# A graph attention layer on one core: q of the last node blocks made behind the first gathers, and a new order of the tail

## The chip, the cores and the metric

One core of a Trainium2 chip runs the whole kernel. The metric is the device time of one execution in microseconds (us). Engines are named as in the profile: PE is TensorE (matrix products and transposes), DVE is VectorE, ACT is ScalarE, POOL is GpSimd, SP is SyncE (it only issues DMAs here). The products are fp32; TensorE's granted clock is given as a share of full speed.

## What is computed

The reference, cut to what matters (12,500 nodes of 256 features, 8 heads of 32, 200,000 edges sorted by their destination `dst`):

```python
h = jnp.maximum(_layernorm(x, axis=-1), 0.0)
q = (h @ Wq + bq).reshape(n, HEADS, D)          # k and v alike
logits = einsum('ehd,ehd->eh', q[dst], k[src]) / sqrt(D)
seg_max = segment_max(logits, dst)
expv = exp(logits - seg_max[dst])
attn = expv / segment_sum(expv, dst)[dst]
agg = segment_sum(attn[:, :, None] * v[src], dst)
g = gelu(agg.reshape(n, HID) + (h @ Wskip + bskip))
y = h + g
out = x + layernorm(y) * gamma + beta
```

So every edge needs the k and v rows of its source, which lie anywhere, and the q row of its destination, which comes in order.

## The kernel before, in words

**Projection** (`project`, L157 to L280). The nodes make 98 blocks of 128, in groups of 1, 2, 4, then 5 for most of the way, and 4, 4, 2, 1 at the end. For each block: layer norm and relu give h; two transposes (L141) and ScalarE's copy to hT (L143); two products of 128x512 for k and v (L258) and their bias addition on VectorE (L261); two products of 128x256 for q (L264) and their bias addition (L268). q is kept as a rounded high part (L269, ScalarE) and the rest (L270, POOL). SP stores each group into three tables in DRAM: h_tab and kv_tab (L273), q_pc (L275). Between these steps VectorE makes a plan of the walk from `dst` (`make_plan`, its last operations L687 to L691).

**Walk over the edges** (`walk_streams`, L768 to L1507). The edges are cut into 8 streams, which advance side by side in NST = 66 steps; a step takes 3 tiles of 128 edges of each stream (the last step 2). Step c does this:

- `gather` (L1058): POOL issues one indirect DMA per stream and tile, 128 rows of kv_tab of 2 KB each: 24 in a step, 1576 in all. They go into tiles of two steps, `rows[c % 2]`; tiles are taken in an order of their own (`ORDER`, 1, 0, 2) when c % 4 is 2 or 3. The gathers of step c + 2 are issued during step c (`gather_next`) and are paced behind VectorE's operations.
- `windows` (L1044 to L1050): SP loads the q rows that the 8 streams can meet in this step from q_pc, at addresses read at run time, 8 loads. `prefetch` (L1030) and `penalties` (L1036) load the step's one-hot codes (et) and masks (pen).
- `hot_e` (L1075, L1077) makes 0/1 matrices of edges against window rows on TensorE and ScalarE, `spread` (L1098) multiplies them with the window, so that each edge has its q.
- On VectorE, `times` (L1107, in two halves) multiplies q by the gathered k, `total` (L1114) adds up over each head; `turn` (L1122, TensorE) turns the logits, `maxima` (L1133 to L1136) takes the segment maxima along the streams, `exponent` (L1140) is on ScalarE, `turn_back` (L1149) on TensorE. `weigh` (L1162 to L1169, VectorE) multiplies v by the weights: only then is a gathered tile free again.
- `hot_n` (L1086, L1088) and the sums (`add_up` and its parts, L1192 to L1216) add the weighted v per node on TensorE; they go to a table.

Pairs of node blocks whose edges are complete are finished meanwhile (`Pair`): `fetch` of sums, x and h; `turn` (L858, L861: h turned); `skip` (L874, L878: h times Wskip); `divide` (L850 to L867); `add` (L883); `gelu` (L887); `stats` (L890 to L896); `root` (L900); `factors` (L904, L905); `normal` (L910); `shifted` (L917, L920: the bias and x); `scale` (L924, L926); `store` by SP (L931) or `store_aside` by POOL (L938). Gelu and Sqrt need different tables of ScalarE; `table_of` (L1010) loads one.

**What sets the order.** In `walk_streams`, nearly every instruction goes through `keep`, which chains it behind the instruction kept before it on its engine. The order in the source is the order on each engine. Ahead of the loop over steps, the source issues the loads of et and pen for step 0, windows(0), the loads for step 1, the 24 gathers of step 0, windows(1), et of step 2, the 24 gathers of step 1, and then the work of step 0. The last two steps, a = 64 and b = 65, are written out after the loop (L1340 to L1496), with the pair blocks that remain: `older`, `before`, `pair` and `late` (class Pair), and four of class Last (`lasts`), which use free halves of gathered tiles as their room.

Of the kernel before, what the change touches and what calls it, by code (L numbers as in the profile page):

```python
# [71 lines left out]
def gnn_kernel(ctx: ExitStack, tc: tile.TileContext, x, src, dst, Wq, bq, Wk, bk, Wv, bv,  # L72
# [83 lines left out]

    def project():  # L157
# [8 lines left out]
        sizes = [1] * NBLK  # L166
        if NBLK >= 14:
            mid = NBLK - 14
            sizes = [1, 2, 4] + [5] * (mid // 5) + [mid % 5] * (mid % 5 > 0) + [4, 2, 1]
        with tc.tile_pool(name="proj_c", bufs=1) as cpool, \  # L170
# [16 lines left out]
            starts = [sum(sizes[:i]) for i in range(len(sizes))]  # L187
# [12 lines left out]
            qscale = 1.0 / math.sqrt(D)  # L200
# [33 lines left out]
            for g, (b0, n) in enumerate(zip(starts, sizes)):  # L234
# [18 lines left out]
                qp = pool.tile([P, 5, 2, HID], F32R, name="qp")[:, :n]  # L253
                for b in range(n):
# [6 lines left out]
                    nc.vector.tensor_tensor(kvo[:, b, :], ps_kv, b_kv, op=OP.add)  # L261
                    ps_q = psum.tile([P, HID], F32, name="ps_q", bufs=1)
# [9 lines left out]
                for tab, t in ((h_tab, h), (kv_tab, kvo)):  # L272
                    nc.sync.dma_start(tab[b0 * P:(b0 + n) * P, :]  # L273
                                      .rearrange("(p b) d -> p b d", p=P), t)
                nc.sync.dma_start(q_pc[b0 * P:(b0 + n) * P, :]  # L275
                                  .rearrange("(p b) d -> p (b d)", p=P),
                                  qp.rearrange("p b k d -> p (b k d)").bitcast(F32))
# [72 lines left out]
    with tc.If(fits > 0) as branch:  # L350
        table = dram.tile([S, NT, KV], F32, name="table")
        walk_streams(tc, N, HID, NST, KL, many, ident, idx, d0_row, slot_row, near, near_n, e_tab, pen_tab,
                     h_tab, kv_tab, q_pc, table, x, out, w_s, one_row, b_s3, b_o3, gam, eps)
    with branch.Else():
        gtab = dram.tile([NP + P, SUMS + HEADS], F32, name="gtab")
        q_tab = dram.tile([NP, HID], F32, name="q_tab")
        queries(q_tab)
# [65 lines left out]
def make_plan(tc, pool, ep, psum, src, dst, N, LEN, NST, SLACK, NT, dram, ident, flag, idx, d0_row,  # L423
# [9 lines left out]
    def behind(ins, share):  # L433

        tc.add_manual_dep(ins.ins, biased[len(biased) * share // 100].ins.name,
# [332 lines left out]
def walk_streams(tc, N, HID, NST, KL, many, ident, idx, d0_row, slot_row, near, near_n, e_tab, pen_tab, h_tab,  # L768
                 kv_tab, q_pc, table, x, out, w_s, one_row, b_s3, b_o3, gam, eps):
# [206 lines left out]
    with ExitStack() as es:  # L976
# [250 lines left out]
        prefetch(0)  # L1227
        penalties(0)
        windows(0)
        prefetch(1)  # L1230
        penalties(1)
        for c in range(2):
            for j in range(tiles_of(c)):
                gather(c, j)
            if c == 0:
                windows(1)
                prefetch(2)
# [132 lines left out]
        lasts = [last(rest[0], spare, 1, True), last(rest[1], kv[1], 0, False),  # L1370
# [37 lines left out]
        lasts[1].fetch_rows()  # L1408
        lasts[2].fetch_rows()
        for half in range(2):  # L1410
            times(b, 1, half)
        total(b, 1)
        pair.skip()
        turn(b, 1)
        weigh(a, 0)
        lasts[3].fetch_rows()
        late.turn()
        late.skip()
        weigh(a, 2)
        maxima(b)  # L1420
        add_up_products(a, 0, (0,))
        add_up_products(a, 1, (1, 0))
        exponent(b)
        before.stats()
        add_up(a, 0, (2,))
        add_up_products(a, 2, (1, 0))
        turn_back(b)
        add_up(a, 1, (2,))
        add_up(a, 2, (2,))
        carried(b)  # L1430
        for j in range(2):
            hot_n(b, j)
        lasts[0].turn()
        lasts[0].skip()
        weigh(b, 1)
        pair.divisors()
        pair.divide()
        pair.add()
        for i in range(3):
            add_up_products(b, i, (1,))  # L1440
        table_of(AF.Gelu)
        pair.gelu()
        weigh(b, 0)
        for i in range(3):
            add_up(b, i, (0,))
        for p in lasts:
            p.fetch_sums()
        late.divisors()
        late.divide()
        late.add()  # L1450
        late.gelu()
        pair.stats()
        lasts[1].turn()
        lasts[1].skip()
        late.stats()
        table_of(AF.Sqrt)
        ends = (before, pair, late)
# [4 lines left out]
        for p in ends:  # L1462
            p.normal()
        lasts[2].turn()
        lasts[2].skip()
        for i, p in enumerate(ends):
            p.shifted()
            p.scale()
            p.store_aside()
            if i == 0:  # L1470
                lasts[3].turn()
                lasts[3].skip()
# [379 lines left out]
```

## Time and profile before

| | us |
|---|---|
| runs shown | 2437.38, 2433.07, 2431.04 (median 2433.07) |
| profiled execution | 2429.78 |
| its span, first to last instruction | 2428.1 |
| TensorE, VectorE, ScalarE, POOL busy | 1697.2, 1996.9, 1061.4, 1664.4 |
| first gather starts, last gather starts | 338.75, 2334.74 |
| last gelu ends | 2402.36 |

The profile is that of one execution. It has a page of groups (engine, line, count, busy time, mean of one, and the idle time of the engine ahead of them with what ended it), slices of the span, and a chain of waits that is followed back from the last instruction. Timelines list start, length and instruction; "issue" is time in which an engine waited for nothing that the profile shows. x8 on a TensorE row counts records: an fp32 product has two. The row "POOLq" or "SPq" is the engine's sequencer, which issues DMAs.

### The profile page before, as it was taken

The numbers are of one execution on the slowest core, as the hardware profiler recorded it, in microseconds if no ns is written. First come the engines' busy times: TensorE is split into PE (matmuls) and PEld (weight loads), VectorE is DVE, ScalarE is ACT, GpSimd is POOL, SyncE is SP. The second block draws the span as 40 slices with busy tenths as digits, with TensorE's granted clock in tenths as the row PEclk, the third lists the DMA queues.
The fourth block names the chain that finished last, engine by engine and source line by source line (L and its number), as shares of the span: only waits on it lengthen the run. The fifth ranks groups of instructions, "written<-read, shape, count | busy, mean of one in ns | idle before, by whom it ended". The sixth has DMA issues, their size and how long they took to land.

```text
span 2428.1 us, 29469 instructions
## 1 busy us (share of the span) xinstructions
PE 1697.2 (70%) x7824; PEld 904.4 (37%) x7824; DVE 1996.9 (82%) x2461; ACT 1061.4 (44%) x2323; POOL 1664.4 (69%) x1751
## 2 busy tenths in 40 slices
PE   6999974555556766667667777676777677667685
PEld 3555532222233333333333333333333333334343
DVE  7579946777788888888988888888888888988873
ACT  4333322333334545545545545455454455455443
POOL 4433547777777777777777777777777777777730
PEclk9999975666667777766767767677677677776666
DMA  7776678888888888988888888888888889988961
GB/s 272 293 265 260 235 257 249 255 256 255 255 269 275 285 279 286 285 274 285 286 284 280 280 291 279 276 285 285 279 281 275 285 270 285 295 269 285 291 189 56
DMA packets 305551, 649.32 MB, mean 267 GB/s; under 512 B 52836, under 2 KB 191470, under 8 KB 300378
## 3 DMA queue, kind: packets, MB, share of 16 engines
q0 software_dynamic: 129056, 424.02, 55.7%
q1 hardware_dynamic: 175570, 222.67, 27.1%
q8 instruction: 64, 1.05, 0.2%
q14 instruction: 113, 0.93, 0.1%
q10 hardware_dynamic: 748, 0.66, 0.1%
HBM read 538.91 MB, written 108.23 MB: 267 GB/s over the span
## 4 chain that ended last, share of the span: by engine, by line
DMA 27%; PE 22%; DVE 18%; issue 12%; POOL 11%; ACT 7%; SPq 3%; DVEq 0%; another core or an unknown queue 0%; POOLq 0%; ACTq 0%
DMA kv<-kv_tab,idx 18%; POOL kv L1058 10%; PE ps_kv L258 5%; DVE kv L1107 4%; DVE vw L1162 4%; PE ps_a L878 4%; DVE L L1114 4%; PE ps_q L264 3%; DMA h<-h_tab 3%; PE ps_qe L1098 2%; DMA out_dram<-o 2%; PE ps_a L1192 1%; DMA sums<-table 1%; PE ps_hot L920 1%; SPq L845 1%
## 5 line engine op out<-in xcount | busy, mean ns | idle before, releaser
L1058 POOL DMA_INDIRECT kv<-kv_tab,idx x1576 | 1517.3, 963 | 482.6 <-issue 339.2
L1107 DVE TENSOR_TENSOR kv<-ps_qe,kv 128x1024 f32<-128x1024 f32 x394 | 470.7, 1219 | 213.8 <-DMA kv<-kv_tab,idx 140.3
L1114 DVE TENSOR_REDUCE L<-kv 128x64 f32<-128x2048 f32 x197 | 450.4, 2286 | 6.9 <-DVE kv L1107 0.2
L1162 DVE TENSOR_TENSOR vw<-ps_x,kv 128x2048 f32<-128x2048 f32 x197 | 449.4, 2281 | 3.6 <-PE ps_x L1149 2.7
L1098 PE MATMUL ps_qe<-qw,to_e 64*128 64x256 f32 (+1 forms) x1576 | 310.2, 392 | 108.9 <-DVE kv L1107 105.8
L1077 ACT ACTIVATE to_e<-ps_hot,ones 128x384 fp32r<-128x384 f32 x396 | 210.5, 573 | 316.3 <-PE ps_hot L1075 307.8
L1098 PEld LDWEIGHTS ps_qe<-qw,to_e 64*128 64x128 f32 (+1 forms) x1576 | 221.8, 246 | 274.4 <-DVE kv L1107 168.5
L1192 PE MATMUL ps_a<-vw,to_n 128*32 128x264 f32 (+1 forms) x2344 | 276.5, 504 | 0.0
L1122 PE MATMUL ps_x<-ident,L 128*64 128x128 f32 x197 | 72.7, 369 | 281.4 <-DVE vw L1169 210.7
L1206 ACT COPY sums_w<-ps_a 128x264 f32<-128x264 f32 x129 | 48.8, 379 | 482.1 <-PE ps_a L1192 426.7
L1075 PE MATMUL ps_hot<-et,near 48*128 48x384 bf16 x396 | 142.5, 420 | 126.8 <-ACT to_e L1077 122.3
L258 PE MATMUL ps_kv<-w_kv,hT 128*128 128x512 f32 x392 | 192.4, 612 | 16.0 <-ACT hT L143 15.0
L270 POOL TENSOR_TENSOR qp<-qp 128x256 fp32r<-128x256 f32 x98 | 96.3, 983 | 154.7 <-ACT qp L269 154.4
L878 PE MATMUL ps_a<-w_s,hT 128*128 128x256 f32 x352 | 164.6, 648 | 19.5 <-ACT hT L861 16.7
L1192 PEld LDWEIGHTS ps_a<-vw,to_n 128*32 128x32 f32 (+1 forms) x2344 | 99.6, 139 | 197.1 <-issue 161.4
L1122 PEld LDWEIGHTS ps_x<-ident,L 128*64 128x64 f32 x197 | 24.7, 126 | 374.6 <-DVE vw L1169 300.6
L1212 ACT COPY kv<-ps_a 1x264 f32<-1x264 f32 x388 | 143.0, 369 | 6.4
L1192 PE MATMUL ps_hot<-vw,to_n 128*64 128x264 f32 x808 | 139.4, 494 | 0.0
L878 PEld LDWEIGHTS ps_a<-w_s,hT 128*128 128x128 f32 x352 | 110.5, 329 | 65.7 <-ACT hT L861 41.8
L1010 ACT ACT_TABLE_LOAD x101 | 129.6, 1283 | 1.7
L1088 ACT ACTIVATE to_n<-ps_hot,ones 128x384 f32<-128x384 f32 x197 | 103.7, 578 | 53.4 <-PE ps_hot L1086 51.2
L264 PE MATMUL ps_q<-w_q,hT 128*128 128x256 f32 x392 | 103.1, 386 | 8.3 <-DVE qp L268 8.2
(288 smaller groups left out, 2111.8 us busy)
## 6 DMA issues: line engine op xcount, KB each, us to landing
qw<-q_pc SPq DMA_DIRECT2D x264, 128.0 KB
kv<-kv_tab,idx POOLq DMA_INDIRECT x1576
kv_tab<-kvo SPq DMA_DIRECT2D x16, 1280.0 KB
q_pc<-qp SPq DMA_DIRECT2D x16, 1280.0 KB
qw<-q_pc SPq DMA_DIRECT2D x264, 64.0 KB
table<-sums_w SPq DMA_DIRECT2D x260, 61.9 KB
pen<-pen_tab SPq DMA_DIRECT2D x66, 192.5 KB
sums<-table SPq DMA_DIRECT2D x90, 132.0 KB
```

Of the source, the lines that this page charges most:

```text
L258: ins = nc.tensor.matmul(ps_kv, hT[:, c, :], w_kv[:, c, :], start=c == 0, stop=c == KC - 1)
L264: ins = nc.tensor.matmul(ps_q, hT[:, c, :], w_q[:, c, :], start=c == 0, stop=c == KC - 1)
L878: self.keep(nc.tensor.matmul(self.ps[:, b, :], self.hT[:, b, c, :], w_s[:, c, :], start=False, stop=False, skip_group_check=True))
L1058: ins = keep(nc.gpsimd.indirect_dma_start(out=t[:, s, :], out_offset=None, in_=kv_tab[:, :], in_offset=bass.IndirectOffsetOnAxis(ap=idx[:, ...
L1075: keep(nc.tensor.matmul(ps[:, :CH], near[:, i * P:(i + 1) * P], step[c]["et"], start=True, stop=True))
L1077: keep(nc.scalar.activation(step[c]["to_e"][:, i, :], ps[:, :CH], AF.Relu, scale=-1.0, bias=ones))
L1098: keep(nc.tensor.matmul(ps[:, b, a, :], g["to_e"][at:at + w, i, j * P:(j + 1) * P], g["qw"][at:at + w, i, :], start=True, stop=True))
L1107: keep(nc.vector.tensor_tensor(k, g["qe", half].rearrange("p b a d -> p a b d"), k, op=OP.mult))
L1114: keep(nc.vector.tensor_reduce(g["L"][:, j, :].rearrange("p (s h) -> p s h", s=S), g["kv"][j][:, :, :HID].rearrange("p s (h d) -> p s h d" ...
L1162: keep(nc.vector.tensor_tensor(t[:, :, HEADS:].rearrange("p s (h d) -> p s h d", h=HEADS), wj[:, :, :, None].to_broadcast([P, S, HEADS, D] ...
L1192: keep(nc.tensor.matmul(ps[at:at + w, :], g["to_n"][:, j, i * P + at:i * P + at + w], g["vw"][j][:, s, :], start=j == turns(c)[0], stop=j ...
L1212: keep(nc.scalar.copy(step[c + 1]["kv"][0][0:1, s, HID - HEADS:], ps[at:at + 1, :]))
```

## The change

Two parts.

**A.** The products of q for the blocks from LATE on are taken out of `project`. A new function `late_queries` makes them inside `walk_streams`, after the 48 gathers of steps 0 and 1 have been issued: it loads Wq and bq again, and for each pair of blocks loads h from h_tab, turns it, multiplies, adds the bias, splits high part and rest, and stores both to q_pc. windows(0), windows(1) and prefetch(2) come after it; et and pen of steps 0 and 1 are loaded within it. It uses the room of the pairs (`sums`, `h`, `hT`, `x_f`, `o`) and the TensorE banks of `hot_e` and `spread`.

**B.** In the written-out tail, the weighings and sums of step a move ahead of the last products of step b; `pair.skip` and the turns and skips of `late` and `lasts` move behind the turned weights of b or behind b's sums; the pair `before` is finished earlier, with one more table load.

The diff, cut to its core (left out: the function's passing to the other branch of `tc.If`, the shifting of `sizes` and `starts`, and an index in the plan's order that stays the same):

```diff
+    LATE = next((b for b in starts if b >= NBLK - 24 and (NBLK - b) % 2 == 0), NBLK)
+    qscale = 1.0 / math.sqrt(D)
+    def late_queries(tile, transposed_ps, product_ps, keep, meanwhile=lambda: None):
+        w_q = tile("sums", KC * HID).rearrange("p (c n) -> p c n", c=KC)
+        b_q = tile("sums", HID)
+        keep(nc.sync.dma_start(w_q, Wq.rearrange("(c p) n -> p c n", p=P)))
+        keep(nc.sync.dma_start(b_q, bass.AP(tensor=bq.tensor, offset=bq.offset,
+                                            ap=[[0, P], [1, HID]])))
+        pairs = range(LATE, NBLK, 2)
+        def fetched(b0):
+            h = tile("h", 2 * HID).rearrange("p (b d) -> p b d", b=2)
+            keep(nc.sync.dma_start(h, h_tab[b0 * P:(b0 + 2) * P, :]
+                                   .rearrange("(p b) d -> p b d", p=P)))
+            return h
+        def transposes(h):
+            ps = transposed_ps()
+            for b in range(2):
+                for c in range(KC):
+                    keep(nc.tensor.transpose(ps[:, b, c, :], h[:, b, c * P:(c + 1) * P], ident))
+            return ps
+        ahead = [fetched(b0) for b0 in pairs[:2]]
+        meanwhile()
+        for t in (w_q, b_q):
+            keep(nc.vector.tensor_scalar(t, t, qscale, None, op0=OP.mult))
+        turned = [transposes(ahead.pop(0))] if ahead else []
+        for i, b0 in enumerate(pairs):
+            hT = tile("hT", 2 * KC * P).rearrange("p (b c d) -> p b c d", b=2, c=KC)
+            keep(nc.scalar.copy(hT, turned.pop()))
+            if i + 1 < len(pairs):
+                turned.append(transposes(ahead.pop(0)))
+            ps = product_ps()
+            for b in range(2):
+                for c in range(KC):
+                    keep(nc.tensor.matmul(ps[:, b, :], hT[:, b, c, :], w_q[:, c, :],
+                                          start=c == 0, stop=c == KC - 1))
+            hi = tile("x_f", 2 * HID).rearrange("p (b d) -> p b d", b=2)
+            lo = tile("o", 2 * HID).rearrange("p (b d) -> p b d", b=2)
+            keep(nc.vector.tensor_tensor(lo, ps, b_q[:, None, :].to_broadcast([P, 2, HID]),
+                                         op=OP.add))
+            keep(nc.scalar.copy(hi.bitcast(F32R), lo))
+            keep(nc.vector.tensor_tensor(lo.bitcast(F32R), lo, hi, op=OP.subtract))
+            if i + 2 < len(pairs):
+                ahead.append(fetched(pairs[i + 2]))
+            for k, t in enumerate((hi, lo)):
+                keep(nc.sync.dma_start(q_pc[b0 * P:(b0 + 2) * P, k * HID:(k + 1) * HID]
+                                       .rearrange("(p b) d -> p b d", p=P), t))
...
-                qp = pool.tile([P, 5, 2, HID], F32R, name="qp")[:, :n]
+                if b0 < LATE:
+                    qp = pool.tile([P, 5, 2, HID], F32R, name="qp")[:, :n]
...
+                    if b0 >= LATE:
+                        continue
...
-                nc.sync.dma_start(q_pc[b0 * P:(b0 + n) * P, :]
-                                  .rearrange("(p b) d -> p (b d)", p=P),
-                                  qp.rearrange("p b k d -> p (b k d)").bitcast(F32))
+                if b0 < LATE:
+                    nc.sync.dma_start(q_pc[b0 * P:(b0 + n) * P, :]
+                                      .rearrange("(p b) d -> p (b d)", p=P),
+                                      qp.rearrange("p b k d -> p (b k d)").bitcast(F32))
...
-        prefetch(0)
-        penalties(0)
-        windows(0)
-        prefetch(1)
-        penalties(1)
         for c in range(2):
             for j in range(tiles_of(c)):
                 gather(c, j)
-            if c == 0:
-                windows(1)
-                prefetch(2)
+        def of_fin(name, n):
+            shape = {"sums": [P, 2, SUMS], "hT": [P, 2, KC, P]}.get(name, [P, 2, HID])
+            t = fin.tile(shape, F32, name=name, bufs=1 if name == "hT" else 2)
+            return t.rearrange("p a b c -> p (a b c)" if name == "hT" else
+                               "p a b -> p (a b)")[:, :n]
+        def first_loads():
+            for c in range(2):
+                prefetch(c)
+                penalties(c)
+        late_queries(of_fin, lambda: hot_ps.tile([P, 2, KC, P], F32, name="ps_hot"),
+                     lambda: qe_ps.tile([P, 2, 2, HID], F32, name="ps_qe")[:, 0], keep, first_loads)
+        windows(0)
+        windows(1)
+        prefetch(2)
...
-        lasts = [last(rest[0], spare, 1, True), last(rest[1], kv[1], 0, False),
+        lasts = [last(rest[0], spare, 1, False), last(rest[1], kv[1], 0, False),
                  last(rest[2], kv[1], 1, False), last(rest[3], kv[0], 0, False)]
         pair.ps_o = bank
 
...
         pair.turn()
         late.fetch_sums()
         lasts[1].fetch_rows()
+        weigh(a, 0)
+        add_up_products(a, 0, (0,))
+        add_up_products(a, 1, (1, 0))
+        weigh(a, 2)
+        add_up(a, 0, (2,))
+        add_up_products(a, 2, (1, 0))
+        add_up(a, 1, (2,))
+        add_up(a, 2, (2,))
         lasts[2].fetch_rows()
+        carried(b)
         for half in range(2):
             times(b, 1, half)
         total(b, 1)
-        pair.skip()
+        for j in range(2):
+            hot_n(b, j)
         turn(b, 1)
-        weigh(a, 0)
-        lasts[3].fetch_rows()
-        late.turn()
-        late.skip()
-        weigh(a, 2)
         maxima(b)
-        add_up_products(a, 0, (0,))
-        add_up_products(a, 1, (1, 0))
         exponent(b)
         before.stats()
-        add_up(a, 0, (2,))
-        add_up_products(a, 2, (1, 0))
         turn_back(b)
-        add_up(a, 1, (2,))
-        add_up(a, 2, (2,))
-        carried(b)
-        for j in range(2):
-            hot_n(b, j)
-        lasts[0].turn()
-        lasts[0].skip()
+        pair.skip()
         weigh(b, 1)
+        for i in range(3):
+            add_up_products(b, i, (1,))
+        table_of(AF.Sqrt)
+        before.root()
+        before.factors()
+        before.normal()
         pair.divisors()
         pair.divide()
-        pair.add()
-        for i in range(3):
-            add_up_products(b, i, (1,))
+        weigh(b, 0)
         table_of(AF.Gelu)
-        pair.gelu()
-        weigh(b, 0)
         for i in range(3):
             add_up(b, i, (0,))
+        lasts[3].fetch_rows()
         for p in lasts:
             p.fetch_sums()
         late.divisors()
         late.divide()
+        pair.add()
+        pair.gelu()
+        before.shifted()
+        late.turn()
+        late.skip()
         late.add()
         late.gelu()
+        before.scale()
+        before.store_aside()
         pair.stats()
-        lasts[1].turn()
-        lasts[1].skip()
+        lasts[0].turn()
+        lasts[0].skip()
         late.stats()
         table_of(AF.Sqrt)
-        ends = (before, pair, late)
+        ends = (pair, late)
         for p in ends:
             p.root()
         for p in ends:
             p.factors()
         for p in ends:
             p.normal()
+        lasts[1].turn()
+        lasts[1].skip()
+        pair.shifted()
+        pair.scale()
+        pair.store_aside()
+        lasts[0].divisors()
+        lasts[0].divide()
+        lasts[0].add()
+        late.shifted()
         lasts[2].turn()
         lasts[2].skip()
-        for i, p in enumerate(ends):
-            p.shifted()
-            p.scale()
-            p.store_aside()
-            if i == 0:
-                lasts[3].turn()
-                lasts[3].skip()
-            elif i == 1:
-                lasts[0].divisors()
-                lasts[0].divide()
-                lasts[0].add()
+        lasts[3].turn()
+        lasts[3].skip()
+        late.scale()
+        late.store_aside()
```

More of the change, by code (lines that the diff above doesn't have):

```diff
@@ L155, in norm_stats @@
         nc.vector.reciprocal(rstd, rstd)
+    sizes = [1] * NBLK
+    if NBLK >= 14:
+        mid = NBLK - 14
+        sizes = [1, 2, 4] + [5] * (mid // 5) + [mid % 5] * (mid % 5 > 0) + [4, 2, 1]
+    starts = [sum(sizes[:i]) for i in range(len(sizes))]
+    LATE = next((b for b in starts if b >= NBLK - 24 and (NBLK - b) % 2 == 0), NBLK)
[44 more added lines that the diff above has]
+                                       .rearrange("(p b) d -> p b d", p=P), t))
@@ L164, in behind @@
                 mybir.DependencyClass.NoSync, mybir.DependencyReason.DATA), reason="kept order")
[L166 to L169, printed above, removed]
         with tc.tile_pool(name="proj_c", bufs=1) as cpool, \
@@ L185, in load @@
                 return xt
-            starts = [sum(sizes[:i]) for i in range(len(sizes))]
             x_in = [load(0, sizes[0])]
@@ L199, in project @@
             rows(b_q, bq)
-            qscale = 1.0 / math.sqrt(D)
             def prepare(g):
@@ L352, in gnn_kernel @@
         walk_streams(tc, N, HID, NST, KL, many, ident, idx, d0_row, slot_row, near, near_n, e_tab, pen_tab,
-                     h_tab, kv_tab, q_pc, table, x, out, w_s, one_row, b_s3, b_o3, gam, eps)
+                     h_tab, kv_tab, q_pc, late_queries, table, x, out, w_s, one_row, b_s3, b_o3, gam, eps)
     with branch.Else():
@@ L356, in gnn_kernel @@
         q_tab = dram.tile([NP, HID], F32, name="q_tab")
+        with tc.tile_pool(name="lq", bufs=2) as pool, \
+                tc.tile_pool(name="lq_ps", bufs=2, space=PSUM) as psum:
+            late_queries(lambda name, n: pool.tile([P, n], F32, name="l_" + name),
+                         lambda: psum.tile([P, 2, KC, P], F32, name="ps_lt"),
+                         lambda: psum.tile([P, 2, HID], F32, name="ps_lq"), lambda ins: ins)
         queries(q_tab)
@@ L433, in behind @@
     def behind(ins, share):
-        tc.add_manual_dep(ins.ins, biased[len(biased) * share // 100].ins.name,
+        tc.add_manual_dep(ins.ins, biased[min(len(biased) - 1, (N // P + 1) * share // 100)].ins.name,
                           mybir.DependencyInfo(mybir.DependencyClass.NoSync,
@@ L768, in walk_streams @@
 def walk_streams(tc, N, HID, NST, KL, many, ident, idx, d0_row, slot_row, near, near_n, e_tab, pen_tab, h_tab,
-                 kv_tab, q_pc, table, x, out, w_s, one_row, b_s3, b_o3, gam, eps):
+                 kv_tab, q_pc, late_queries, table, x, out, w_s, one_row, b_s3, b_o3, gam, eps):
     nc = tc.nc
```

## The prediction, made before the changed kernel ran

> **What bounds the kernel now.** I read the page first: the slices (part 2), then the groups of instructions (part 5). The walk over the edges is most of the span.
>
> ```profile
> span 2428.1 us, 29469 instructions
> ...
> PEclk9999975666667777766767767677677677776666
> ...
> L1058 POOL DMA_INDIRECT kv<-kv_tab,idx x1576 | 1517.3, 963 | 482.6 <-issue 339.2
> ```
>
> A gather takes POOL 0.96 us, with about 0.3 us of its own issue behind it: a pitch of 1.2575 us, 30.2 us for the 24 of a step. 1576 x 1.2575 = 1982 us of the 1996 between the first gather (338.75) and the last (2334.74). VectorE has some 25 us of work per step. So the walk has the length of its gather stream: **a start that moves moves the end, and a stall of the stream is never made good.** What counts is when gather 1 starts, whether one later waits, and how long the tail is.
>
> The start, from the chain of waits:
>
> ```profile
> 332.42 0.72 POOL qp L270
> 333.15 1.88 issue
> 335.02 0.77 POOLq L349
> 335.79 0.02 issue
> 335.81 1.79 DMA q_pc<-qp
> 337.60 1.12 another core or an unknown queue
> 338.72 0.03 POOLq L1848
> 338.75 0.65 POOL kv L1058
> ```
>
> Gather 1 (called G below) follows the last store of q. The 48 gathers of steps 0 and 1 have buffers of their own. Gather 49 takes the buffer of tile 1 of step 0 (ORDER is 1, 0, 2), so it needs weigh(0,1). The timelines of POOL and VectorE:
>
> ```profile
> 398.82 0.95 POOL L1058 DMA_INDIRECT kv<-kv_tab,idx  x1 [0.30 <-issue]
> ```
> ```profile
> 347.85 1.23 DVE L1107 TENSOR_TENSOR kv<-ps_qe,kv 128x1024 f32<-128x1024 f32 x1 [11.44 <-DMA kv<-kv_tab,idx]
> ...
> 386.76 0.22 DVE L1169 COPY vw<-ps_x 128x64 f32<-128x64 f32 x1
> ```
>
> Gather 49 starts at its own pitch, G+60; weigh(0,1) had ended at 386.98, G+48. The slack is 12 us.
>
> What the late queries will meet is the DMA view of 342 to 354 us:
>
> ```profile
> DMA packets 2336, 3.63 MB, mean 302 GB/s; under 512 B 361, under 2 KB 1832, under 8 KB 2335
> ...
> q0 software_dynamic: 623, 2.06, 55.2%
> q1 hardware_dynamic: 1712, 1.56, 46.0%
> ```
>
> The engines are full, and SP's queue gets 1.56 MB in 12 us, **130 GB/s**. The table by stretches gives 338 to 354 and 360 to 400 us:
>
> ```profile
> 338.00:354.00 16.00, 10.07 (x24) 4.04 (x24) 1.71 (x2) 6.31 (x12) 11.98 (x13) 0.51 0.90 267
> 360.00:400.00 40.00, 13.68 (x56) 7.55 (x60) 26.95 (x20) 5.70 (x12) 30.32 (x32) 0.50 0.79 241
> ```
>
> The last three columns are granted clock, DMA share, GB/s: TensorE runs at half clock there.
>
> **Part A: q of 16 blocks.** The words say 24, but the code takes the first group start from 74 on with an even rest. The starts are 72, 77, 82, so LATE is 82: 16 blocks, 8 pairs.
>
> Removed from the projection: 4 products of 128x256 for each pair. A pair takes 6.17 us (its first product at 322.43, the next pair's at 328.60 in TensorE's rows); in the chain of waits the two of one block take 0.86, so four 1.72. TensorE is busy through that stretch, so 8 x 1.72 = 13.8 us. The q stores go as well: the last kv_tab store, issued at 333.92, comes at about 320.5, lands 1.8 later, and gather 1 follows in 1.1: G' = 323.4. That is **15 us earlier** (13 to 15.5, if the bias additions of VectorE, already close behind, hold up a pair).
>
> Added behind gather 48's issue, with SP's and the compute engines' orders written out: Wq and bq again (384 KB), and per pair one h load of 256 KB and two q stores of 256 KB, 786 thousand bytes. ScalarE's written order is hT copy, cast, next hT copy, and the cast needs the addition of this pair's product: the pairs form a chain of hT copy 0.59 (L861), product 1.99 at full clock or 3.78 at half (L878 has the same shape and both durations in the tail), addition 0.69 (L890's shape), cast some 0.63 (as L861), hand-overs some 0.3: 4.2 to 6.0 us a pair. Transposes and the subtraction lie beside it. By bytes: 786 KB at 130 GB/s is 6.0 us, at 150 5.2. I take **5.6 us a pair** (ends 4.2, the chain at full clock, and 7.1, 110 GB/s).
>
> Windows(0) reads q_pc at addresses known only at run time, so it now waits for all these stores: an added wait. Behind it on SP stand windows(1) and prefetch(2), behind those spread(0), all of VectorE's work on step 0, and gather 49. SP's penalties and prefetches for 0 and 1 move ahead of it and cost nothing there. Time line from G':
>
> - Weights and two h loads, 896 KB at 150 GB/s: first product at +6.
> - Seven pairs more: 7 x 5.6 = 39.2, so +45.2.
> - Last pair's product, addition, cast, subtraction, two issues and the landing (1.79 above): 8.5, +53.7.
> - windows(0) to first multiplication: in the profile 338.60 to 347.85, 9.3: **+63**.
> - VectorE from there to the end of weigh(0,1), all gathers long landed: tile 0 1.2+1.2+2.3; tile 1 1.2+1.8+1.2+2.3; tile 2 4.7; 0.6 wait; maxima 2.5; step 1's first tile 4.7; weigh 2.5: 26.5 us.
>
> Gather 49 wants to go at +60.4, so the first multiplication must start by +33.9. It starts 29 us too late, and POOL stands still for 29. **Part A: -15 + 29 = +14 us.** Low end: pairs at 4.2 and short ends (first product +4, 6 to the last landing, 6 for the windows, whose eight loads took 4.53 to issue) give +45, stall 11.5, sum -3.5. High end: 7.1 a pair, 11 for the windows, give +75, stall 41, sum +26.
>
> The Trainium skill's page "DMA: Bandwidth & Descriptors", section "Queues, rings and completion order", speaks against this part: each DMA engine takes its queues in turn, packet by packet, so a queue of loads and stores laid under a gather stream is not free. The row of q0 and q1 above agrees in kind (55% and 46%). By half of that page's 358 GB/s per core ("Specifications"), an estimate, a pair would take 4.4 us, not the 6.0 of the row, and part A would come to some +4. By the rows I stay at +14.
>
> **Part B: the tail.** The last gather lands by 2339.87. VectorE waited for it, then for others (its timeline):
>
> ```profile
> 2339.87 1.23 DVE L1107 TENSOR_TENSOR kv<-ps_qe,kv 128x1024 f32<-128x1024 f32 x1 [2.83 <-DMA kv<-kv_tab,idx]
> 2341.13 2.29 DVE L1114 TENSOR_REDUCE L<-kv 128x64 f32<-128x2048 f32 x1
> 2344.33 2.29 DVE L1162 TENSOR_TENSOR vw<-ps_x,kv 128x2048 f32<-128x2048 f32 x1 [0.91 <-PE ps_x L1122]
> ...
> 2355.28 2.29 DVE L1162 TENSOR_TENSOR vw<-ps_x,kv 128x2048 f32<-128x2048 f32 x1 [2.69 <-PE ps_x L1149]
> ```
>
> The two weighings of step a (2 x 2.4 us) move ahead of the last products. They fill the 2.83 us wait and push the products about 2.2 back; behind them maxima comes at about 2346.2 (was 2349.12), and weigh(b,1) at 2349.8 instead of 2355.28. But the pair's skip products, which filled TensorE during 2340 to 2344, and the late pair's turn and skip (2345 to 2351) go behind turn_back, into the stretch in which TensorE sets the end: from 2355.2 to 2401.7 it has 27.4 us of full-clock work in 46.5, 10 of them idle. After the change: from about 2349, 32.1 us of full-clock work x 1.32 (this stretch's slowing by the clock) + 7 idle = 49, last gelu near 2398 instead of 2402.4. One more change of ScalarE's table (1.28) lies beside the sums. The stores behind the last gelu stay. **Part B: -4 us** (-7, if all 5.5 us survive and idle time shrinks; +3, if the moved 5 us run at half clock with the old gaps).
>
> **Sum:** 2429.8 (the profiled execution, 1.7 us outside its span) + 14 - 4 = 2439.8. The median of the runs shown is 2433.1, 3.3 higher, so on its footing **2443**.
>
> **Rivals.**
> 1. *About even* (2433, from 2426 to 2440). Pairs at 4.3 to 5.2 us, since gathers leave SP's queue more than in 342 to 354: stalls of 15 to 25. For it: DMA was not full in 360 to 400, 0.79. Against: until gather 48 the gathers alone ask for 262 KB per 1.2575 us, 208 GB/s of the 302 seen.
> 2. *The other side: faster* (2425.5). The gathers yield to SP's queue, which gets 190 GB/s: the chain at full clock sets 4.2 a pair, with the short ends; A -3.5, B -4. For it: gathers 9 to 48 are in no hurry, since only gather 49 sets the end; TensorE had full clock up to 338. Against: 130 GB/s and 0.50 as soon as the gathers ran. Part A turns to a gain once the first multiplication starts before +49, which with short ends is below 4.7 us a pair, with the ends of the main case below 3.6.
> 3. *Much slower* (2459). SP's queue gets 110 GB/s, A +26, B 0. For it: h and q rows of 1 KB beside gathered rows of 2 KB, if the queues take turns by packet.
> 4. *The tail loses*: the moved skips run at half clock and set the end, B +3; with part A as forecast 2450.
>
> **Chances.** Main case 0.38, rival 4 0.09, rival 3 0.10, even 0.30, faster 0.13. A measurement of this kernel tells about 0.3% from no change, 7.3 us. So faster 0.13, same 0.30, slower 0.57. The range, 2425 to 2459, runs from rival 2 to rival 3 and leaves out the half of each that lies beyond, and the tail's ends on top of them.
>
> **What would show it.** Right: gather 1 near 323.4; first multiplication near G'+63 waiting for windows; POOL idle by some 29 us before gather 49, no other gap; projection pairs at 4.45 us. Wrong: idle time under 15 us (pairs quicker than 4.7 us), a gather stream slower than 1.2575 per gather while SP's queue is full, or a projection held by VectorE instead. In the tail: weigh(b,1) 11.5 us after the last gather's landing instead of 15.4, last gelu about 58 after it instead of 62.5.

## The result and the profile after

The changed kernel took 2451.8 us (median of 6 runs, 2444.44 to 2452.75) beside 2432.06 for the kernel before on the same chip (2426.9 to 2437.38): a ratio of 1.0068, 95% interval 1.0054 to 1.0081. By the ratio that is 16.5 us slower (13 to 20; the two medians lie 19.7 apart), where 10 were forecast; the time lies in the stated range. The profiled execution has a span of 2450.4 us, 22.3 more than the one before. One later run (the eleventh below) was taken while the kernel before itself took 2982.84 us, 23% more than here, and is compared with that time alone.

The lines of the changed kernel are 61 further down in the walk: gathers are L1119, `times` L1168, `weigh` L1223 and L1230.

The page, with the groups' columns (busy us, mean ns of one, then idle time ahead of them):

```profile
span 2450.4 us, 29587 instructions
...
PEclk9999985666667677767767766677767766677677
...
L1119 POOL DMA_INDIRECT kv<-kv_tab,idx x1576 | 1521.2, 965 | 531.7 <-issue 369.1
```

The gathers are as many and as long as before; their idle time is 49 us more. POOL's timeline has it in two places, ahead of gather 1 (18.78 us, POOL done with the plan; before: 2.58) and of gather 49:

```profile
326.01 1.05 POOL L1119 DMA_INDIRECT kv<-kv_tab,idx  x1 [18.78 <-issue]
...
386.11 0.95 POOL L1119 DMA_INDIRECT kv<-kv_tab,idx  x1 [0.30 <-issue]
420.15 0.95 POOL L1119 DMA_INDIRECT kv<-kv_tab,idx  x1 [33.09 <-DVE vw L1230]
```

Gather 1 starts 12.4 us earlier than before (338.36 in POOL's rows; the 338.75 of the chain of waits is a later piece of the same gather). Gather 49 starts 21.3 us later (398.82), after 32.8 us in which POOL only waits for weigh(0,1): "DVE vw L1230" is that weighing's last instruction. SP and VectorE show why it is late:

```profile
383.35 0.53 SPq L212 DMA_DIRECT2D q_pc<-o  x1
387.83 9.70 SPq L1111 DMA_DIRECT2D qw<-q_pc  x16
```
```profile
392.61 1.23 DVE L1168 TENSOR_TENSOR kv<-ps_qe,kv 128x1024 f32<-128x1024 f32 x1 [9.29 <-PE ps_qe L1159]
...
417.61 2.28 DVE L1223 TENSOR_TENSOR vw<-ps_x,kv 128x2048 f32<-128x2048 f32 x1
419.80 0.21 DVE L1230 COPY vw<-ps_x 128x64 f32<-128x64 f32 x1
```

The last late store is issued at 383.35; the window's loads stand behind it until it has landed (387.83); the first multiplication is at 392.61, 66.6 us after gather 1 (before: 9.5). From there VectorE takes 27.4 us to the end of weigh(0,1).

The DMA view of 342 to 354 us, the stretch shown of before:

```profile
DMA packets 2000, 4.02 MB, mean 335 GB/s; under 512 B 248, under 2 KB 1105, under 8 KB 2000
...
q0 software_dynamic: 799, 2.62, 64.2%
q1 hardware_dynamic: 1201, 1.40, 32.4%
```

SP's queue now gets 1.40 MB in 12 us, 117 GB/s. The gathers get 218, more than the 208 that their pitch asks for: in this stretch they do not yield.

### The profile page after: what moved, and what is told of

The parts are those of the page before. It is cut to its first block, busy times and chain, and to the rows that moved or that the text cites. A ratio compares the mean times of both kernels' runs of the same rounds, so it can differ in the third digit from the quotient of the medians.

```text
span 2450.4 us, 29587 instructions
## 1 busy us (share of the span) xinstructions
PE 1713.4 (70%) x7856; PEld 911.6 (37%) x7856; DVE 2002.7 (82%) x2463; ACT 1064.7 (43%) x2325; POOL 1650.8 (67%) x1735
## 3 DMA queue, kind: packets, MB, share of 16 engines
q1 hardware_dynamic: 180770, 225.16, 27.4%
## 4 chain that ended last, share of the span: by engine, by line
DMA 27%; PE 20%; DVE 19%; issue 13%; POOL 10%; ACT 7%; SPq 2%; DVEq 0%; POOLq 0%; ACTq 0%
DMA kv<-kv_tab,idx 20%; POOL kv L1119 10%; PE ps_kv L311 5%; DVE kv L1168 5%; DVE vw L1223 4%; DVE L L1175 3%; PE ps_a L939 3%; DMA h<-h_tab 3%; PE ps_qe L1159 2%; PE ps_q L319 2%; PE ps_a L1253 2%; ACT L1071 1%; DMA out_dram<-o 1%; DMA sums<-table 1%; PE ps_hot L981 1%
## 5 line engine op out<-in xcount | busy, mean ns | idle before, releaser
L1119 POOL DMA_INDIRECT kv<-kv_tab,idx x1576 | 1521.2, 965 | 531.7 <-issue 369.1
L1168 DVE TENSOR_TENSOR kv<-ps_qe,kv 128x1024 f32<-128x1024 f32 x394 | 469.8, 1217 | 192.4 <-DMA kv<-kv_tab,idx 103.9
L1223 DVE TENSOR_TENSOR vw<-ps_x,kv 128x2048 f32<-128x2048 f32 x197 | 449.3, 2280 | 0.7 <-ACT ps_x L1185 0.7
L1183 PE MATMUL ps_x<-ident,L 128*64 128x128 f32 x197 | 72.4, 367 | 278.6 <-DVE vw L1230 205.3
L939 PE MATMUL ps_a<-w_s,hT 128*128 128x256 f32 x352 | 165.5, 651 | 22.4 <-ACT hT L922 19.7
L325 POOL TENSOR_TENSOR qp<-qp 128x256 fp32r<-128x256 f32 x82 | 79.4, 968 | 131.3 <-ACT qp L324 131.1
L1183 PEld LDWEIGHTS ps_x<-ident,L 128*64 128x64 f32 x197 | 24.7, 125 | 371.7 <-DVE vw L1230 293.4
L1253 PE MATMUL ps_hot<-vw,to_n 128*64 128x264 f32 x808 | 146.4, 514 | 0.0
L939 PEld LDWEIGHTS ps_a<-w_s,hT 128*128 128x128 f32 x352 | 110.6, 329 | 68.3 <-ACT hT L922 44.4
L311 PEld LDWEIGHTS ps_kv<-w_kv,hT 128*128 128x128 f32 x392 | 71.2, 192 | 78.2 <-issue 48.7
```

Of the source, the lines that this page charges most:

```text
L311: ins = nc.tensor.matmul(ps_kv, hT[:, c, :], w_kv[:, c, :], start=c == 0, stop=c == KC - 1)
L939: self.keep(nc.tensor.matmul(self.ps[:, b, :], self.hT[:, b, c, :], w_s[:, c, :], start=False, stop=False, skip_group_check=True))
L1119: ins = keep(nc.gpsimd.indirect_dma_start(out=t[:, s, :], out_offset=None, in_=kv_tab[:, :], in_offset=bass.IndirectOffsetOnAxis(ap=idx[:, ...
L1168: keep(nc.vector.tensor_tensor(k, g["qe", half].rearrange("p b a d -> p a b d"), k, op=OP.mult))
L1223: keep(nc.vector.tensor_tensor(t[:, :, HEADS:].rearrange("p s (h d) -> p s h d", h=HEADS), wj[:, :, :, None].to_broadcast([P, S, HEADS, D] ...
L1253: keep(nc.tensor.matmul(ps[at:at + w, :], g["to_n"][:, j, i * P + at:i * P + at + w], g["vw"][j][:, s, :], start=j == turns(c)[0], stop=j ...
```

## The experiments

Stated before them: **the theory** is the forecast's, that the late pairs delay step 0 past the point at which gather 49 needs its buffer, and that each pair's pace is the bytes that SP's queue gets. **Rivals**: the loss lies in the tail or the walk; the pace is the latency of the h loads, with two in flight; the wait of windows(0) for the stores alone holds step 0; the late queries have a fixed cost. Ratios are to the kernel before, with 95% intervals. "First times" and "stall" are read from each profile, the first in us after gather 1.

| run | late blocks | ratio | gather 1 | first times | stall at gather 49 |
|---|---|---|---|---|---|
| before | 0 | 1 | 338.36 | 9.5 | 0 |
| after | 16 | 1.0068 (1.0054 to 1.0081) | 326.01 | 66.6 | 32.8 |
| e1 A alone | 16 | 1.0098 (1.0082 to 1.0113) | 322.95 | 67.8 | 32.8 |
| e2 B alone | 0 | 0.998 (0.9969 to 0.9991) | 338.64 | 10.4 | 0 |
| e3 A, 8 blocks | 8 | 1.0028 (1.0014 to 1.0042) | 331.04 | 43.7 | 11.7 |
| e4 A, h loaded ahead | 16 | 1.0079 (1.0063 to 1.0096) | 323.82 | 61.3 | 29.8 |
| e5 A, window first | 16 | 1.0069 (1.0043 to 1.0096) | 324.56 | 73.0 | 38.3 |
| e6 A and B, interleaved | 16 | 1.0031 (1.0018 to 1.0044) | 324.39 | 16.4 | 22.6, and 6.7 later |
| e7 B, turn first | 0 | 0.9972 (0.9959 to 0.9984) | 340.10 | 9.5 | 0 |
| e8 4 blocks, turn first | 4 | 0.9966 (0.9953 to 0.9978) | 334.87 | 30.7 | 0 |
| e8b 6 blocks, turn first | 6 | 0.9967 (0.9952 to 0.9981) | 333.70 | 35.5 | 3.8 |
| e9 staged | 12 | 0.9957 (0.994 to 0.9974) | 328.89 | 13.2 | 0; 2.1 and 8.3 later |
| e10 staged (the eleventh run) | 8 | 1.0017 (0.9996 to 1.0038) | 335.18 | 17.0 | 26.3, and many later |
| e11 staged, again | 8 | 0.9946 (0.9932 to 0.9959) | 333.51 | 16.6 | 0 |

**Each part by itself (e1, e2).** e1 has the changed kernel's start and the tail of before; e2 the other halves.

```diff
 # against the changed kernel: behind the loop, the lines of before
-        weigh(a, 0)
-        add_up_products(a, 0, (0,))
...
+        pair.skip()
+        turn(b, 1)
+        weigh(a, 0)
...
```

> Part A alone, with the tail of before. Theory (the late queries hold step 0 back and the gather stream loses more than it won): in the profile of the changed kernel gather 1 came 12.7 us earlier and gather 49 21.3 us later, so this kernel should show the same two shifts and take 20 to 24 us more than before. Rival (the loss lies in the tail or in the walk's pitch, and the two shifts at the start are made good later): within 8 us of before.

> Part B alone, with the start of before. Theory (the tail is 2 to 5 us shorter: the last gelu came 62.4 us after the last gather's start instead of 67.6, of which the eight output stores, 17.5 us instead of 14.5, took back 3): 2 to 5 us less than before. Rival (the longer chain of stores belongs to the new order and eats the whole gain): no change, 0 to +2 us.

e1 took 2455.7 us beside 2432.99, by the ratio 23.8 more (20 to 27.5); e2 2428.03, 4.9 less (2.2 to 7.5). Their sum, +18.9, meets the 16.5 of both within the intervals. So the loss is part A's, and part B is a gain. That the longer chain of stores belongs to the new order falls: in e2 the eight output stores are issued within 14.8 us, in before 14.5. It goes with the late blocks instead: the profiles without them (before, e2, e7) have 14.5 to 14.8, all others 15.0 to 17.5, e1 with the tail of before 16.7. No run shows why. e1's profile is of a run of 2446.72 us, the other five took 2453 to 2457: in it gather 49 is 19.5 us late, so some of the 23.8 stands in no profile.

**How many late blocks (e3).**

```diff
-        sizes = [1, 2, 4] + [5] * (mid // 5) + [mid % 5] * (mid % 5 > 0) + [4, 2, 1]
+        sizes = [1, 2, 4] + [5] * (mid // 5) + [3, 5, 2, 1]
...
-    LATE = next((b for b in starts if b >= NBLK - 24 and (NBLK - b) % 2 == 0), NBLK)
+    LATE = next((b for b in starts if b >= NBLK - 8 and (NBLK - b) % 2 == 0), NBLK)
```

> Part A with 8 late blocks, 4 pairs, instead of 16 (the last groups are 3, 5, 2, 1 instead of 4, 4, 2, 1, LATE is 90), tail of before. Theory (each late pair past a certain number costs its whole pace of 6.35 us and wins only 1.72): first multiplication at 8.1 + 3 x 6.35 + 9.3 + 4.8 = 41 us after gather 1, the stream stands for 8 us instead of 33, gather 1 comes 6 us earlier than in before: 1 to 3 us more than before, some 18 less than part A alone. Rival (a fixed cost of the late queries, such as their weights, the window load behind the stores or the order of the queue, makes the stall): stall over 20 us, 14 us or more above before.

Measured 6.8 us above before (3.4 to 10.2), where 1 to 3 were expected, and 16 below e1. The stall shrank from 32.8 to 11.7 us for four pairs less, 5.3 a pair, while the start came 8.1 us later, 2.0 a pair. Between 8 and 16 blocks a late pair costs more than it wins; a fixed cost isn't needed. The sum itself was missed by some 3 us: 43.7 instead of 41 to the first multiplication, and 11.7 instead of 8 of stall. Most of that is the window's load, 7.3 us from issue to first multiplication while gathers were still issued, where the sum had 4.8.

**Bytes or latency (e4).** All eight h loads are issued ahead, into tiles of the weighted v that nobody uses yet.

```diff
-        ahead = [fetched(b0) for b0 in pairs[:2]]
+        ahead = [fetched(b0) for b0 in pairs[:depth]]
...
+            if name == "h":
+                if not rooms:
+                    r = work.tile([P, S, SUMS], F32, name="vw", bufs=K).rearrange(
...
+                return rooms.pop(0)
```

> Part A with all eight h loads issued ahead, into room of the weighted v that is not in use yet, instead of two in flight; tail of before. Theory as predicted (the pace of 6 us a pair is the bytes that SP's queue gets beside the gathers): the same bytes, pace 5.5 to 6.4, time within 5 us of part A alone. Rival, from the trace of the changed kernel (each h load took 10 to 15 us from issue to its transposes and two were in flight, so the latency of the loads sets the pace): pace 4.2 to 5 us, first multiplication 9 to 14 us earlier, time 9 to 14 us below part A alone.

Between the two. The pace from first to last cast fell from 6.37 us in the changed kernel to 5.18. VectorE's additions in e4, one for each pair:

```profile
346.56 0.69 DVE L205 TENSOR_TENSOR o<-ps_qe,sums 128x512 f32<-128x512 f32 x1 [5.88 <-DMA q_pc<-o]
...
352.26 0.69 DVE L205 TENSOR_TENSOR o<-ps_qe,sums 128x512 f32<-128x512 f32 x1 [3.63 <-PE ps_qe L201]
...
357.96 0.69 DVE L205 TENSOR_TENSOR o<-ps_qe,sums 128x512 f32<-128x512 f32 x1 [3.63 <-PE ps_qe L201]
...
361.87 0.69 DVE L205 TENSOR_TENSOR o<-ps_qe,sums 128x512 f32<-128x512 f32 x1 [1.84 <-PE ps_qe L201]
...
365.78 0.69 DVE L205 TENSOR_TENSOR o<-ps_qe,sums 128x512 f32<-128x512 f32 x1 [1.84 <-PE ps_qe L201]
```

With h at hand the distance is 5.7 us where the products ran at half clock (3.78 us) and 3.91 where at full (1.99): the chain of the forecast, not the bytes. Only the first row waits for a transfer, the store that still reads its buffer. Nor was SP's queue at its most in the changed kernel: 4 to 14 us after gather 1 it got 182 GB/s in e4, with the eight loads under way, beside 195 of the gathers (328 to 338 us), but 105 beside 240 in the changed kernel (330 to 340 us).

In the changed kernel TensorE waited for h instead. SP issues the loads of pairs 4, 5 and 6, and TensorE begins their transposes, at:

```profile
339.43 0.59 SPq L177 DMA_DIRECT2D h<-h_tab  x1
...
345.71 0.58 SPq L177 DMA_DIRECT2D h<-h_tab  x1
...
352.52 0.56 SPq L177 DMA_DIRECT2D h<-h_tab  x1
```
```profile
345.95 1.09 PE L185 MATMUL ps_hot<-ident,h 128*128 128x128 f32 x4 [3.02 <-DMA h<-h_tab]
...
351.49 0.63 PE L185 MATMUL ps_hot<-ident,h 128*128 128x128 f32 x4 [1.74 <-DMA h<-h_tab]
...
358.43 0.63 PE L185 MATMUL ps_hot<-ident,h 128*128 128x128 f32 x4 [4.58 <-DMA h<-h_tab]
```

That is 6.5, 5.8 and 5.9 us from issue, 5.8 to 6.5 for pairs 3 to 8. The 10 to 15 us of the expectation arise when each row of transposes is counted from the load issued one before its own. The row at 345.95 is pair 4's: that at 332.19 (x8) holds pairs 1 and 2, and pair 3's starts at 339.15, before the load of 339.43 is issued. So a load takes some 6 us, and what makes it late is the written order. On SP the load of pair 4 stands behind the stores of pair 1, that of pair 6 behind those of pair 3. On TensorE the transposes of pair 4 stand ahead of the products of pair 3. That closes a loop: load of pair 4, products of pair 3, their addition, cast, subtraction and stores, load of pair 6. One turn makes two pairs and took 10.9 to 13.6 us between issues (333.31, 345.71, 356.63 and 339.43, 352.52, 366.15), in the mean 12.5, or 6.3 a pair. e4 opens the loop by issuing all loads first. Moving the load ahead of the stores on SP alone was not run.

But the gain did not reach gather 49 in full: the first multiplication came 6.5 us earlier, the stall 3 us shorter, the median 5 us lower, all against e1 (the intervals still touch). In e4 the window's loads ran beside the last gathers: 7.2 us from issue to first multiplication instead of e1's 4.8, and VectorE then waited 3.8 us for the second half.

**The wait alone (e5).** windows(0) goes ahead of the late stores.

```diff
                 penalties(c)
+            windows(0)
...
-        windows(0)
         windows(1)
```

> Part A alone, but windows(0) is loaded ahead of the late stores, so that step 0 does not wait for them (right only for lists as these, where the last stream's first windows lie ahead of the late blocks). Theory that the wait of windows(0) for the stores is the loss: first multiplication some 30 us earlier, nearly no stall, time 10 to 15 us below before. Rival: on TensorE, ScalarE and VectorE the late pairs themselves stand ahead of step 0 in the written order, so that step 0 waits for the last of them with or without the wait: only the last landing and the load of the window go, 5 to 10 us (383 to 392.6 in the changed kernel), less the 4.5 us by which the window's loads push the h loads back: 2 to 7 us below part A alone.

VectorE's timeline, with the last late pair and the first multiplications:

```profile
393.08 0.69 DVE L205 TENSOR_TENSOR o<-ps_qe,sums 128x512 f32<-128x512 f32 x1 [3.63 <-PE ps_qe L201]
394.45 0.69 DVE L208 TENSOR_TENSOR o<-o,x_f 128x512 fp32r<-128x512 f32 x1 [0.68 <-ACT x_f L207]
397.52 2.37 DVE L1168 TENSOR_TENSOR kv<-ps_qe,kv 128x1024 f32<-128x1024 f32 x2 [2.37 <-PE ps_qe L1159]
```

The loads of step 0's q rows were all issued by 337.3 us, and step 0 still starts behind the last pair's subtraction. So the order on the engines is enough to hold it, and the wait of windows(0) is not needed for it. The size was a miss: the window's eight loads on SP (8.64 us of issue) pushed the third h load to 337.98, the first multiplication came at 73.0 instead of earlier, and the stall grew to 38.3. The time, 16.8 us above before by the ratio (10.5 to 23.3), can't be told from e1's.

**The late pairs between step 0's tiles (e6).**

```diff
             turn(0, j)
+            late(2)
...
+            if c == 0:
+                late(2)
+                windows(2)
```

> Both parts, with windows(0) and (1) loaded ahead of the late stores and the late pairs put between the work of step 0: two behind each of its three tiles, two behind its first weighing; windows(2) behind the last store; the products go into the bank of the sums (right only for lists as these, as in the run before). Theory (the 16 blocks' work is small, some 11 us of VectorE, and only its place ahead of step 0 costs): gather 1 at 323 to 326, gather 49 waits 0 to 6 us, time 12 to 20 us below before. Rival (the work itself delays weigh(0,1), since TensorE at half clock and loads of 12 us each stand in line with step 0): stall of 15 us or more, no gain or a loss against part B alone.

Two whole pairs come behind each tile. The rival held. The first multiplication is at 16.4, but gather 49 waits 22.6 us, since VectorE stands in line for each pair's products:

```profile
366.41 2.29 DVE L1177 TENSOR_REDUCE L<-kv 128x64 f32<-128x2048 f32 x1
374.57 0.69 DVE L204 TENSOR_TENSOR o<-ps_a,sums 128x512 f32<-128x512 f32 x1 [5.88 <-PE ps_a L200]
```

Of the rival's two reasons the half clock is seen: from 352 to 400 us five of six pairs' products take TensorE 3.5 to 3.8 us, the sixth 1.99, and none of its waits there is for a load of h. The time is 7.5 us above before (4.4 to 10.7), part B's gain included.

**The staged pairs (e9, e11).** Each pair is cut into three stages that stand one tile apart: turn, products, and the rest.

```diff
+        for k in range(n + 2):
+            if 0 <= k - 2 < n:
+                finish(k - 2)      # addition, cast, subtraction, stores
+            if 0 <= k - 1 < n:
+                multiply(k - 1)
+            if k < n:
+                turn_h(k)
...
```

> Both parts with 12 late blocks, 6 pairs (the last groups are 4, 5, 4, 2, 1, LATE is 86), windows(0) and (1) loaded ahead of the late stores as in the interleaved run, and each late pair cut into three stages (turn; products; addition, cast, subtraction and stores) that stand one tile of step 0 or 1 apart, so that VectorE does not wait for the products of a pair; the turn of the last logits ahead of hot_n. Theory (in the interleaved run VectorE stood 30 us ahead of gather 49's release waiting for the products of pairs, not working on them: 3.6 to 5.9 us for each pair against 1.4 us of its own work): stall 0 to 6 us, gather 1 10 us earlier than in before, 8 to 16 us below before. Rival (TensorE at half clock and the load of windows(2) behind the last stores hold steps 1 and 2 instead): gather 49 on time, but later gathers wait 8 us or more.

Gather 49 goes on time (389.39). Ahead of weigh(0,1) VectorE now finishes two pairs without a wait for their products, in e6 six with waits of 1.9 to 5.9 us. That fits the theory, but e9 has fewer pairs, later, and in stages, all at once, and no run separates the three. The rival's later wait is there too, in POOL's timeline of e9:

```profile
404.15 0.95 POOL L1137 DMA_INDIRECT kv<-kv_tab,idx  x1 [2.37 <-DVE kv L1186]
...
422.47 0.95 POOL L1137 DMA_INDIRECT kv<-kv_tab,idx  x1 [8.57 <-DVE W L1215]
```

and TensorE tells what VectorE waited for, the window of step 2, loaded behind the last store:

```profile
411.75 0.55 PE L1177 MATMUL ps_qe<-qw,to_e 64*128 64x256 f32 x1 [9.28 <-DMA qw<-q_pc]
```

The time is 10.5 us below before (6 to 15). The profile is of a run of 2430.3 us, where the median of six is 2422.27, so the two waits may be longer in it than in the others. With 8 blocks:

> As the staged run, with 8 late blocks, 4 pairs, instead of 12 (the last groups are 3, 5, 2, 1). In the staged run gather 49 went on time, but two later gathers waited 2.1 and 8.3 us, because the load of windows(2) stands behind the last late store (issued at 402.8). Theory: with two pairs less the last store is issued some 11 us earlier, and windows(2) is there when step 2 needs it: no stall over 2 us, gather 1 some 7 us earlier than in before, 11 to 15 us below before. Rival (the stall moves with the order, not with the number of pairs): a stall of 5 us or more, no better than the staged run with 12 blocks.

Its first run took 2987.78 us beside 2982.84: no gain (1.0017, 0.9996 to 1.0038). In its profile gather 49 waits 26.3 us and POOL stands idle for 1064 us ahead of gathers (page of before: 483), so the gather stream no longer sets the length of the walk, as the argument needs. Why that was so is not shown. Once more:

> The staged kernel with 8 late blocks once more, since the kernel before itself took 2983 us beside its first run, in which the gathers waited nearly everywhere. Theory as there: last late store some 11 us earlier than with 12 blocks, no stall over 2 us, gather 1 some 7 us earlier than in before: 11 to 15 us below before. Rival: a stall of 5 us or more behind windows(2), no better than the staged run with 12 blocks.

2419.35 us beside 2432.5: **13.1 us below before** (10 to 16.5), no stall, and better than both kernels. Like e6 and e9 (e5 for windows(0)) it loads windows(0) and (1) ahead of the late stores, which is right only where the last stream's first windows lie ahead of the late blocks, as here.

**Few late blocks, and the turn in the tail (e7, e8, e8b).** In e7 (part B) and in the rest the turn of the last logits goes ahead of hot_n:

```diff
         total(b, 1)
+        turn(b, 1)
         for j in range(2):
             hot_n(b, j)
-        turn(b, 1)
         maxima(b)
```

> Part B alone, with the turn of the last logits (step b, tile 1) ahead of hot_n of b on TensorE. Theory (in part B the maxima of b came 14.2 to 15.7 us after the last gather's start, no earlier than before's 14.4, because the turn stands behind hot_n, which waits for ScalarE's copies of the sums): maxima 1.5 to 2.5 us earlier against the last gather; since TensorE sets the rest of the tail, the time 0 to 2 us below part B alone. Rival (TensorE's sums of step a alone hold the turn): maxima within 0.5 us of part B alone.

> Both parts with only 4 late blocks, 2 pairs (the last groups are 4, 3, 3, 1, LATE is 94), and the turn of the last logits ahead of hot_n. Theory (the late pairs are free until the first multiplication passes 33.9 us after gather 1; with 8 blocks it came at 43.7, and each pair is 6.35): first multiplication at 31, stall 0 to 1 us, gather 1 some 3.9 us earlier than in before: 3 to 4 us below part B with the turn, 8 to 11 below before. Rival (the late queries have a fixed cost that even two pairs pay): stall of 4 us or more, no better than part B with the turn.

> As the run with 4 late blocks, but 6, 3 pairs (the last groups are 5, 3, 2, 1, LATE is 92). Theory: first multiplication at 37.3 after gather 1, stall 4 to 6 us, gather 1 5.6 us earlier than in before: within 2 us of part B with the turn, so worse than 4 blocks by some 4 us. Rival (a fixed cost): as for 4 blocks, and no difference between the two.

e7: maxima 10.7 us after the last gather's start instead of e2's 15.7, more than expected; but the other kernels with this turn have 10.6 to 14.2, so one profile does not size it. The wait itself is removed: VectorE's idle time just ahead of the maxima is 0.39 us in e7, e8, e8b, e9 and e11, all with this turn, against 3.77 in the changed kernel, 1.92 in e2 and 2.07 in e6. The time (6.8 us below before, 3.9 to 10; e2 4.9) does not tell a gain beyond part B, so that is left open. e8 and e8b: with 4 blocks no stall, with 6 one of 3.8 us, as expected; so a fixed cost that stalls the stream is excluded. Their times (8.3 and 8.0 us below before) are equal, where 4 us between them were expected: the start differs by 1.2 us, the stall by 3.8, and the walk and tail of single runs scatter by as much.

## Why the prediction held, and where its sums were off

**Right in its main mechanism, wrong in one overlap.** It named the earlier start, a stall of the gather stream ahead of gather 49 alone, the 16 blocks instead of 24, and a shorter tail. But the measured 2451.8 lies about midway between its 2443 and the 2459 of "much slower", and part A by itself (+23.8) lies by that rival's +26, not by +14. Its terms against the profile after:

| term | forecast | measured |
|---|---|---|
| gather 1 earlier | 15 | 12.4 here, 13.8 to 15.4 in e1, e4, e5, e6 |
| first product after gather 1 | 6 | 8.1 |
| seven pairs more | 39.2 (5.6 each) | 44.4 (6.35 each) |
| last product to the window's issue | 8.5 | 9.3 |
| window's issue to first multiplication | 9.3 | 4.8 |
| first multiplication to end of weigh(0,1) | 26.5 | 27.4 |
| stall | 29 | 32.8 |
| part A at gather 49 | +14 | +21.3 |
| part A by its own time (e1) | +14 | +23.8 (20 to 27.5) |
| part B by its own time (e2) | -4 | -4.9 (-2.2 to -7.5) |

**The mis-sized term** is the seven pairs. "I take **5.6 us a pair**" mixed two limits, the chain (4.2 to 6.0) and the bytes at 130 to 150 GB/s (5.2 to 6.0). The chain was sized about right where h is at hand: e4 shows 3.9 to 5.7. What failed is the overlap: "Transposes and the subtraction lie beside it". The transposes of the next pair stand ahead of each pair's products on TensorE and waited for h, whose load of some 6 us was issued only behind the stores of an earlier pair. So the load lies in the chain, once for every two pairs, and sets 6.35 us a pair. The windows' load, taken from before's loaded stretch, was too dear by 4.5 us, because the gathers had all been issued by then (last before the stall at 386.11); the two errors nearly cancel, which is luck.

The Trainium skill's page "DMA: Bandwidth & Descriptors", section "Queues, rings and completion order", was right in kind to speak against this part. The even share worked out from its 358 GB/s per core ("Specifications"), an estimate of 179, was not what SP's queue got in the changed kernel (117 in the rows above), but lies close to the 182 that it got in e4 with eight loads under way.

Two slips of the working are small: the parts listed for 26.5 add up to 26.2, and 333.92 less 13.8 is 320.1, not 320.5.

**The added wait** was told as what holds step 0. It does hold windows(0), but e5 shows that it is not needed: the late pairs stand ahead of step 0 in the kept order of three engines, and that holds it by itself.

**The start.** 32 products fewer (two for each of 16 blocks) brought 1.7 us a pair in TensorE's rows (4.44 instead of 6.17); the profile after was already 2.4 us behind where the late blocks begin (a product of the same group at 282.84 us, in before at 280.44), and the other four runs of part A with 16 blocks give the forecast's 15 within 1.2 us.

**The tail.** The forecast's 2.9 us for the maxima did not come in the profile after: 14.2 us after the last gather's start, against 14.4. VectorE and then TensorE:

```profile
2373.41 0.70 DVE L1194 TENSOR_TENSOR_SCAN ps_x<-pen,ps_x 64x256 f32<-64x256 f32 x1 [3.77 <-PE ps_x L1183]
```
```profile
2372.82 0.32 PE L1147 MATMUL ps_hot<-near_n,et 48*128 48x384 bf16 x1 [0.74 <-ACT kv L1273]
2373.07 0.30 PE L1183 MATMUL ps_x<-ident,L 128*64 128x128 f32 x1
```

The turn (L1183) stands behind hot_n (L1147), which waits for ScalarE's copies of the sums: a wait in the place of the one removed, which the prediction didn't name. weigh(b,1) still came 2.9 us earlier (17.6 against 20.5) and the last gelu 5.3 (62.35 against 67.6), near the forecast's -4. The end gained only 2.2 in this one profile, since the eight output stores, each behind the landing of the one ahead, were issued over 17.5 us instead of 14.5; in e2 they were not. A single profile does not size this: from the last gather's start to the end of the span the tail of before takes 93.4 us in its own profile and 89.0 to 91.9 in e1, e3, e4 and e5, the new one 91.2 here and 85.4 and 86.3 in e2 and e6.

**Rivals.** "Much slower" was right in direction, and its A of +26 lies in e1's interval; but 7.1 us a pair was not reached (6.35), part B did gain, and so 2459 was not reached. "Faster" failed at the point that it gave: 4.7 us a pair was not reached as a mean, with 6.4 in the changed kernel and 5.2 in e4, though there the gathers did leave SP's queue 182 GB/s for a while. "About even" ended at 2440. "The tail loses" is excluded by e2.

## What to carry to other kernels

Work taken off the path ahead of a stream that issues without pause is only a gain if it is done before the stream's buffers run out: work out that deadline (here the first multiplication 34 us after gather 1; 30.7 gave no stall, 35.5 a small one) and, for each load in the moved work, not only its bytes but where it is issued and what stands behind it. An engine that runs in a written order is held by the place of moved work as much as by its waits: removing the wait left the stall, and fewer pairs, cut into stages a tile apart, removed it.

## What the runs showed of the hardware

- A 256 KB load on SP's queue took 5.8 to 6.5 us from issue to use while gathers ran (profile after, pairs 3 to 8). SP's queue got 117 GB/s beside the gathers' 218 in 342 to 354 us of it (before: 130 and 172), and 182 beside 195 with eight such loads under way (e4, 328 to 338 us).
- The same window's load took 4.8 us from issue to first multiplication when all gathers had been issued (after, e1) and 7.1 to 7.3 while they still were (e3, e4, e8, e8b).
- The granted clock was 0.72 in 326 to 388 us of the profile after, with TensorE busy for 30.5 of 62 us, and 0.50 in 338 to 398.8 of before, with 25.0 of 60.8:

```profile
326.00:388.00 62.00, 30.48 (x102) 21.35 (x102) 11.96 (x18) 11.98 (x22) 46.72 (x48) 0.72 0.94 311
```

- From gather 49 to the last gather, with no stall after it, the same 1527 gathers took 1935.9 us in before, 1939.0 in after and up to 1943.6 in e3: single profiles differ here by 8 us with no change in the code between.
